# Four graph layers on one core: a POOL clear behind row gathers and scatters, and other chunk orders

## The chip, the core and the metric

The kernel runs on one core of a Trainium2 chip. A core has five engines with queues of their own: PE (TensorE, matrix products), DVE (VectorE), ACT (ScalarE), POOL (GpSimd) and SP (SyncE, which here only issues transfers). Transfers run on 16 DMA engines that all queues share. The metric is device time in microseconds (us) of one execution, as the median over runs.

## The reference

The input is a node matrix x of 3327 x 512 numbers and a 3327 x 3327 0/1 adjacency matrix with about four ones per row. Four layers follow each other; each normalises x, clips it at zero and adds what a graph layer makes of it:

```python
h = jnp.maximum(_layernorm(x, axis=-1), 0.0)
x = x + _L0_gnn_ref(h, adj, ...)   # mean of the neighbours' rows, two products, relu
h = jnp.maximum(_layernorm(x, axis=-1), 0.0)
x = x + _L1_gnn_ref(h, adj, ...)   # attention over neighbours, 8 heads of 64
h = jnp.maximum(_layernorm(x, axis=-1), 0.0)
x = x + _L2_gnn_ref(h, adj, ...)   # attention, 4 heads of 128, elu at the end
h = jnp.maximum(_layernorm(x, axis=-1), 0.0)
x = x + _L3_gnn_ref(h, adj, ...)   # attention, 1 head of 512
```

In an attention layer a node's score against each neighbour is a leaky relu of the sum of two numbers, one of each node; a softmax over the neighbours gives weights, and the node's new row is the weighted sum of the neighbours' projected rows.

## The kernel before

**The load stage** (plan of lines 880 to 1510) streams the adjacency matrix through SBUF, finds each row's ones (`L1209` on DVE), writes lists of neighbours (`records`, `L1261` to `L1267` on POOL), normalises x and multiplies it for layer 0, and sorts the nodes by number of neighbours. At its end 26 indirect transfers from POOL (`scatter`, `L1435`) write the rows in their sorted order to the DRAM table `own`; the records come back as `srec`, and the layers begin.

**The layers.** After the sort, the 3328 node places are 26 chunks of 128. Chunk 0 holds the nodes with most neighbours and has 14 slots, chunk 1 has 8, chunks 2 and 3 have 7, and so on down to chunks 24 and 25 with 1; 117 slots in all. For every slot of a chunk one indirect transfer (`gather`, `L1562`) fetches up to 128 rows of about 2 KB from the layer's DRAM table into the SBUF buffer `ring`, which has room for 33 slots. The table of the next layer is written by `project` (PE product `L1780`, ACT copies, an SP transfer), and no gather of a layer may start before all rows of its table have been written: a one-element clear on POOL (`mark`, `L2222`) waits for them.

Layer 0 sums slots on PE (`L1593`, a product with the identity) and DVE. Layers 1 and 2 compute scores on POOL (`L1942` clears padding, `L1950` adds two numbers for each slot and head), the softmax on DVE and ACT, multiply the slots by their weights in place (`L2138` on DVE, an operation that reads two SBUF operands; some slots on ACT), and sum on PE and DVE. Layer 3 takes its scores on DVE (`L1969`), makes the weighted sum there (`L2058`), projects on PE (`L2088`), and an indirect transfer from POOL (`L2100`) puts 128 finished rows of the output in their original places.

**What sets the order.** Inside the layers every engine's order is written out by a planner (class `Plan`). Each operation has an engine, an estimated cost in us, a rank and the operations it comes after; `run` simulates the engines as queues, takes whatever can start first, and emits the operations in order of their simulated start. The rank is the layer and the place of the chunk's unit in `ORDERS`, a hand-given list of single chunks and pairs for each layer. The engines then run strictly in that order. A gather costs 1.27 us in the planner, a clear of padding 0.15 us a chunk, and a score operation 0.3 us and more. The load stage is planned in the same way, but its last part, the scatters, is emitted after the plan and is placed by an automatic scheduler.

Of the kernel before, what the change touches and what calls it, by code (L numbers as in the profile page):

```python
# [8 lines left out]
F32 = mybir.dt.float32  # L9
# [9 lines left out]
P = 128  # L19
# [7 lines left out]
def general_path(  # L27
# [519 lines left out]
    def l3_finish(pc, i, o):  # L547
# [17 lines left out]
CAPS = tuple(-(-r // 128) for r in ROWS)  # L565
SEG = 4
RING = 33
NEVER = -1.0e30
LIFT = 0.5 ** (1.0 / 3.0)
LOG_LIFT = -0.23104906018664842  # L570
# [6 lines left out]

ORDERS = {
    0: (
        (24,), (12, 21), (11,), (6,), (18,), (17,), (15,), (4,), (3,), (20,), (5, 9), (22,), (10, 19), (1,),  # L580
        (2,), (14,), (0,), (23,), (8,), (13, 16), (7,), (25,),
    ),
    1: (
        (18, 21), (22, 24), (15,), (5,), (10, 20), (2,), (17,), (12, 23), (19,), (4,), (9, 14), (7,), (11, 16),
        (8, 13), (6,), (1,), (0,), (3,), (25,),
    ),
    2: (
        (18, 23), (19, 24), (16,), (20,), (6, 11), (10, 14), (7, 12), (5, 13), (9,), (1,), (21, 22), (4,), (0,),
        (8,), (2,), (3,), (15,), (17,), (25,),
    ),  # L590
    3: (
        (0,), (7,), (17,), (15, 20), (25,), (11,), (3,), (23,), (1, 5), (24,), (4, 14), (16,), (12, 22), (8,),
        (9,), (10,), (18,), (2,), (13,), (19,), (21,), (6,),
    ),
}

# [17 lines left out]
class Plan:  # L614
# [7 lines left out]
        self.limits = limits  # L622
        self.taker = {}

    def add(self, engine, cost, rank, emit=None, after=(), lag=0.0, take=(), give=()):
        op = {
            "engine": engine,
            "cost": cost,
            "rank": (rank, len(self.ops)),
            "emit": emit,  # L630
            "lag": lag,
            "take": take,
            "give": give,
            "need": 0,
            "ready": 0.0,
            "next": [],
        }

        after = list(after)
        for tag in take:  # L640
            if tag in self.taker:
                after.append(self.taker[tag])
            self.taker[tag] = op
        for a in after:
            a["next"].append(op)
            op["need"] += 1
        self.ops.append(op)
        return op

    def run(self):  # L650
        free = {}
        stock = {tag: [0.0] * n for tag, n in self.limits.items()}
        waiting = {}
        for op in self.ops:
            if not op["need"]:
                waiting.setdefault(op["engine"], []).append(op)
        order = []
        while any(waiting.values()):
            best = None
            for engine, ops in waiting.items():  # L660
                for op in ops:
                    at = max(op["ready"], free.get(engine, 0.0))
                    for tag in op["take"]:
                        at = max(at, min(stock[tag])) if stock[tag] else None
                        if at is None:
                            break
                    if at is not None and (best is None or (at, op["rank"]) < best[:2]):
                        best = (at, op["rank"], op)
            at, _, op = best
            waiting[op["engine"]].remove(op)  # L670
            for tag in op["take"]:
                stock[tag].remove(min(stock[tag]))
            op["at"] = at
            end = at + op["cost"]
            free[op["engine"]] = end
            for tag in op["give"]:
                stock[tag].append(end + 0.1)
            for after in op["next"]:
                lag = op["lag"] + (0.1 if after["engine"] != op["engine"] else 0.0)
                after["ready"] = max(after["ready"], end + lag)  # L680
                after["need"] -= 1
                if not after["need"]:
                    waiting.setdefault(after["engine"], []).append(after)
            order.append((at, len(order), op))
        assert len(order) == len(self.ops)
        for _, _, op in sorted(order, key=lambda o: o[:2]):
            if op["emit"]:
                op["emit"]()
        return max(free.values())
# [3 lines left out]
def gnn_stack_kernel(  # L693
# [19 lines left out]
    nc = tc.nc  # L713
# [21 lines left out]
    with ExitStack() as st:  # L735
# [116 lines left out]
        with tc.tile_pool(name="p0", bufs=1) as pa, tc.tile_pool(name="p0p", bufs=2, space=PSUM) as pp:  # L852
# [52 lines left out]
            fidx = pa.tile([P, NK, SEG * 8], U32, tag="fidx", name="fidx")  # L905
# [5 lines left out]
            plan = Plan(limits)  # L911
# [368 lines left out]
            for pos, i in enumerate(SEQUENCE):  # L1280
                found_of[i] = look(pos, i)
                for a, b in LISTED:
                    if i == max(range(a, b), key=pos_of.get):
                        done, rec = lists((ADJ * (pos + 0.9), 1), a, b, [f for k in range(a, b) for f in found_of[k]])
# [147 lines left out]
            landed = []  # L1432

            def scatter(i):
                ins = nc.gpsimd.indirect_dma_start(  # L1435
                    out=own,
                    out_offset=bass.IndirectOffsetOnAxis(ap=box["ranki"][:, i : i + 1], axis=0),
                    in_=node(i),
                    in_offset=None,
                )  # L1440

                for other in scattered:
                    tc.declare_no_dep(ins.ins, other.ins, reason="rows of their own")
                scattered.append(ins)
# [15 lines left out]
            with nc.allow_non_contiguous_dma(reason="each node's record and place beside its row"):  # L1460
# [46 lines left out]

                with tc.manual_schedule():
                    plan.run()
                for i in SEQUENCE:  # L1510
                    scatter(i)
                back()
                degrees()


        with tc.tile_pool(name="run", bufs=1, reuse_waits="tile") as pr, tc.tile_pool(
            name="runp", bufs=2, space=PSUM, reuse_waits="tile"
        ) as pp:
            xres = pr.tile([P, NK, D], F32, tag="xres", name="xres")
            ring = pr.tile([P, RING, WIDE], F32, tag="ring", name="ring")  # L1520
            hsum = {
                layer: pr.tile([P, NK, DC], F32, tag=f"hsum{layer}", name=f"hsum{layer}") for layer in (1, 2, 3)
            }
# [11 lines left out]
            def held(i, s):  # L1535

                return min(P, ROWS[s] - i * P)

            def pool_cost(m):
                return 1.27  # L1540
# [4 lines left out]
            def gather(layer, i, rank, barrier):  # L1545

                S = slots_of[i]
                r0 = ring_at[0] if ring_at[0] + S <= RING else 0
                ring_at[0] = r0 + S
                before = ring_readers[r0 : r0 + S]  # L1550
                last = []
                ring_readers[r0 : r0 + S] = [last] * S
                landed = []
                for s in range(S):

                    def emit(s=s):
                        if layer == 0:
                            idx = srec[:, i, s : s + 1]
                        else:
                            idx = nbr[:, base_of[i] + s : base_of[i] + s + 1]  # L1560
                        m = held(i, s)
                        nc.gpsimd.indirect_dma_start(  # L1562
                            out=ring[:m, r0 + s, : width[layer]],
                            out_offset=None,
                            in_=table[layer],
                            in_offset=bass.IndirectOffsetOnAxis(ap=idx[:m, :], axis=0),
                        )

                    after = barrier + before[s]
                    issue = plan.add("pool", pool_cost(held(i, s)), rank, emit, after)  # L1570
                    landed.append(plan.add("dma", 0.95 * held(i, s) / P, rank, None, [issue], lag=1.3))
                return ring[:, r0 : r0 + S, :], landed, last

# [337 lines left out]
            def attend(layer, number, unit, barrier):  # L1911
# [15 lines left out]
                if soft:  # L1927
# [14 lines left out]
                                nc.gpsimd.memset(e[:, j, full:, :], NEVER)  # L1942

                    if on_pool:
                        score = [plan.add("pool", 0.15 * n, rank, emit, take=("soft",))]
                        for j, i in enumerate(soft):
                            for lo, hi, m in runs_of(i, 0, slots_of[i]):

                                def emit(j=j, i=i, lo=lo, hi=hi, m=m, g=g, box=box):
                                    nc.gpsimd.tensor_tensor(  # L1950
                                        box["e"][:m, j, lo:hi, :],
                                        g[i][:m, lo:hi, D : D + H],
                                        fsrc[layer][:m, i, :].unsqueeze(1).to_broadcast([m, hi - lo, H]),
                                        ALU.add,
                                    )

                                score.append(
                                    plan.add("pool", 0.3 + 0.0015 * (hi - lo) * H, rank, emit, score[:1] + landed[i][lo:hi])
                                )

                    def emit(unit=soft, n=n, S=S, g=g, box=box, small=small, on_pool=on_pool):
# [58 lines left out]
                for j, i in enumerate(unit):  # L2020
# [56 lines left out]
                    if layer == 3:  # L2077
# [28 lines left out]
                                oob_is_err=False,  # L2106
                            )

                        issue = plan.add("pool", 1.3, rank, emit, [done])
                        plan.add("dma", 1.1, rank, None, [issue], lag=1.3, give=("t",))  # L2110
                        continue
                    j = unit.index(i)
# [121 lines left out]
                for number, unit in enumerate(ORDERS[layer]):  # L2234
                    ends += attend(layer, number, unit, barrier)
            with tc.manual_schedule():
                plan.run()


    general = nc.values_load(  # L2240
# [47 lines left out]
```

## Time and profile before

| | |
|---|---|
| median of 13 runs | 1110.13 us (1104.35 to 1112.82) |
| profiled execution | 1109.94 us, of which the span of the trace is 1107.9 us |
| busy, share of the span | PE 79%, DVE 65%, POOL 58%, ACT 47% |
| first gather, layer 0 to 3 | 268.58, 451.78, 680.50, 903.83 us |
| end of the last gather, layer 0 to 3 | 414.89, 635.07, 871.72, 1080.49 us |
| `mark` of layers 1 to 3 | 447.32, 676.50, 903.11 us |

Times inside the trace count from the first instruction. In the list of groups, the numbers after the bar are the busy time of the group, the mean time of one instruction in ns, the time the engine stood idle just before such instructions, and what ended most of that idle time; "issue" there means that the engine waited for nothing that the profile shows. In the list of waits, the three numbers are the total, the number of waits and the longest. In a timeline the numbers are start and duration in us, with idle time before the instruction in brackets.

### The profile page before, as it was taken

What the parts mean: (1) busy time and instruction counts of PE and PEld (TensorE: products, weight loads), DVE (VectorE), ACT (ScalarE), POOL (GpSimd) and SP (SyncE); (2) the same over time, 40 slices, a digit from 0 to 9 for tenths busy, and PEclk for the clock granted to TensorE, in tenths of its full rate; (3) what the DMA queues carried; (4) which work ended last, traced back from release to release, by engine and by line L of the source; (5) the groups of instructions that cost most, each with busy time, mean ns of one, the idle gap of its engine ahead of it and who ended that gap; (6) DMA issues with size and microseconds to landing.
All of it is one profiled execution on the core that took longest, in us unless ns stands there. A gap on an engine that the chain in (4) does not pass through costs nothing. (4 is left out here: it accounts for less than half of the span.)

```text
span 1107.9 us, 11566 instructions
## 1 busy us (share of the span) xinstructions
PE 880.7 (79%) x2853; PEld 498.2 (45%) x2853; DVE 716.4 (65%) x1760; ACT 519.9 (47%) x1700; POOL 643.3 (58%) x807
## 2 busy tenths in 40 slices
PE   7699999993999989388869693787889832949874
PEld 4244444441576757265636452444444431424332
DVE  6499988900869577287789491686767826536541
ACT  4398887530454435164657342455544631313231
POOL 1060444673777770577688703788767427777771
PEclk9899999996999999689999888688878955979988
DMA  9999888298999983467777603667656336677671
GB/s 352 316 355 388 303 304 296 88 358 297 303 335 325 320 273 120 130 181 195 201 193 197 181 30 98 184 179 195 185 159 184 112 102 171 203 201 210 193 209 55
DMA packets 89911, 240.51 MB, mean 217 GB/s; under 512 B 24933, under 2 KB 26477, under 8 KB 89834
## 3 DMA queue, kind: packets, MB, share of 16 engines
q0 software_dynamic: 41600, 137.72, 42.9%
q1 hardware_dynamic: 48234, 101.96, 26.0%
q8 instruction: 25, 0.41, 0.2%
q14 instruction: 52, 0.43, 0.1%
HBM read 190.35 MB, written 49.27 MB: 216 GB/s over the span
## 5 line engine op out<-in xcount | busy, mean ns | idle before, releaser
L1562 POOL DMA_INDIRECT ring<-table,nbr x351 | 379.1, 1080 | 114.4 <-issue 73.2
L1593 PE MATMUL acc<-ring,ident 128*128 128x512 f32 (+1 forms) x494 | 264.0, 671 | 81.3 <-DVE ring L2138 58.0
L1780 PE MATMUL pw<-w,hT 128*128 128x264 f32 (+1 forms) x832 | 195.0, 391 | 14.5 <-ACT hT L1705 14.5
L1780 PEld LDWEIGHTS pw<-w,hT 128*128 128x128 f32 x832 | 159.9, 193 | 55.2 <-ACT hT L1705 21.6
L1593 PEld LDWEIGHTS acc<-ring,ident 128*128 128x128 f32 (+1 forms) x494 | 96.9, 211 | 190.1 <-issue 81.4
L1562 POOL DMA_INDIRECT ring<-table,srec x117 | 111.0, 948 | 46.3 <-issue 20.7
L2138 DVE TENSOR_TENSOR ring<-ring,w 128x2048 f32<-128x2048 f32 (+7 forms) x76 | 114.6, 1534 | 1.7
L1209 DVE FIND_INDEX8 fidx<-one_i,ai 128x8 uint32<-128x832 int32 x104 | 104.2, 1019 | 0.0
L2088 PE MATMUL pw<-w,hT 128*128 128x512 f32 x208 | 96.7, 608 | 5.0 <-ACT hT L2080 5.0
L1217 ACT ACTIVATE junk<-ai 128x1664 int8<-128x1664 int32 (+1 forms) x52 | 82.7, 1591 | 33.0 <-DMA ai<-in_adj_dram 32.7
L1349 PE MATMUL pz_n<-wf,hT_n 128*128 128x512 f32 x208 | 92.3, 595 | 1.4 <-ACT hT_n L1342 1.4
L1349 PE MATMUL py_n<-wf,hT_n 128*128 128x512 f32 x208 | 91.9, 592 | 0.0
L1705 ACT ACTIVATE hT<-pt 128x128 f32<-128x128 f32 (+1 forms) x312 | 82.1, 292 | 19.3 <-PE pt L1694 18.7
L1996 ACT ACTIVATE ex<-el 128x48 f32<-128x48 f32 (+19 forms) x56 | 12.6, 228 | 134.1 <-DVE el L1979 133.7
L1976 DVE SCALAR_TENSOR_TENSOR el<-e 128x48 f32<-128x48 f32 (+19 forms) x56 | 10.3, 185 | 98.3 <-POOL e L1950 88.0
L1705 ACT ACTIVATION_READ_ACCUMULATOR hT<-pt 128x1 f32 x312 | 69.2, 223 | 0.0
L2088 PEld LDWEIGHTS pw<-w,hT 128*128 128x128 f32 x208 | 40.2, 196 | 60.0 <-issue 45.9
L1349 PEld LDWEIGHTS pz_n<-wf,hT_n 128*128 128x128 f32 x208 | 39.0, 190 | 51.1 <-issue 45.9
L822 ACT ACTIVATE ln<-mv,eps 128x1 f32<-128x1 f32 (+1 forms) x60 | 18.1, 302 | 92.9 <-DVE mv L1650 89.3
L2074 PE MATMUL pt<-ident,y 128*128 128x128 f32 x96 | 15.6, 294 | 57.9 <-DVE y L2058 51.5
L2124 ACT ACTIVATE ring<-ring,w 128x64 f32<-128x64 f32 (+1 forms) x216 | 57.7, 357 | 4.0 <-DVE w L2006 3.0
L2058 DVE SCALAR_TENSOR_TENSOR acc<-ring,w,acc 128x512 f32<-128x512 f32 (+2 forms) x67 | 50.5, 754 | 13.6 <-ACT acc L2056 12.0
(187 smaller groups left out, 1279.0 us busy)
## 6 DMA issues: line engine op xcount, KB each, us to landing
ai<-in_adj_dram SPq DMA_DIRECT2D x25, 832.0 KB, 7.1
ai<-in_adj_dram SPq DMA_DIRECT2D x25, 831.5 KB, 7.5
table<-t SPq DMA_DIRECT2D x52, 258.0 KB, 3.2
xy<-own SPq DMA_DIRECT2D x26, 512.0 KB, 5.7
table<-t SPq DMA_DIRECT2D x26, 260.0 KB, 5.7
table<-zt_n SPq DMA_DIRECT2D x26, 256.0 KB, 6.0
ring<-table,nbr POOLq DMA_INDIRECT x351, 3.7
later<-in_x_dram SPq DMA_DIRECT2D x15, 256.0 KB, 6.8
```

The lines of the kernel that those rows point to most:

```text
L822: nc.scalar.activation(ln, var, AF.Ln, bias=eps, scale=scale)
L1209: nc.vector.max_index(fidx[:, i, qq * 8 : (qq + 1) * 8], one_i, ai[:, q * QW : min(cols, (q + 1) * QW)])
L1217: nc.scalar.activation(junk[:, :cols], tiles["ai", key][:, :cols], AF.Square, accum_out=sq[:, i, hf : hf + 1])
L1349: nc.tensor.matmul(pz, tiles["hT", key][:, c, :], wf[s][:, c, :], start=(c == 0), stop=(c == DC - 1))
L1562: nc.gpsimd.indirect_dma_start(out=ring[:m, r0 + s, : width[layer]], out_offset=None, in_=table[layer], in_offset=bass.IndirectOffsetOnAxi ...
L1593: nc.tensor.matmul(acc, ident[:m, :], g[:m, s, :D], start=(k == 0), stop=(k == len(slots) - 1))
L1705: nc.scalar.activation(hT[:, c, :n], pt[:, c, :n], AF.Copy, accum_out=hsum[layer][:, i, c : c + 1])
L1780: nc.tensor.matmul(pw[:, b, :w], tiles["hT", key][:, c, :], wsb[layer][:, c, b, :w], start=(c == 0), stop=(c == DC - 1),)
L2058: nc.vector.scalar_tensor_tensor(to[:m, :], row, weight, acc[:m, :], ALU.mult, ALU.add)
L2088: nc.tensor.matmul(pw[:, 0, :], tiles["hT", key][:, c, :], w3[:, c, :], start=False, stop=(c == DC - 1))
L2124: nc.scalar.activation(v, v, AF.Copy, scale=box["w"][:m, j, s, h : h + 1])
L2138: nc.vector.tensor_tensor(v, v, box["w"][:m, j, lo:hi, :].unsqueeze(3).to_broadcast([m, hi - lo, H, O]), ALU.mult,)
```

## The change

1. A clear of an SBUF tile of 128 x 384 float32 numbers that nothing reads (`spacer`, `GAP`) is emitted on POOL between two operations of the layers' plan that are marked `spaced` and follow each other on POOL: row gathers, and the output's scatters of layer 3. Where a score operation stands between two gathers, no clear is put in.
2. In the source each scatter of the load stage is followed by a clear of the first 12 chunks' part of `fidx`, which has 384 numbers a partition.
3. The planner's cost of a gather or an output scatter goes up by 0.26 us (`SPACE`), and its costs of padding clears and scores on POOL go down.
4. `ORDERS` of all four layers are other permutations with other pairs. Every chunk's own instructions, slots and shapes stay the same.

```diff
+SPACE = 0.26
+GAP = 384
 ORDERS = {
     0: (
-        (24,), (12, 21), (11,), (6,), (18,), (17,), (15,), (4,), (3,), (20,), (5, 9), (22,), (10, 19), (1,),
-        (2,), (14,), (0,), (23,), (8,), (13, 16), (7,), (25,),
+        (24,), (16,), (11,), (21,), (22,), (23,), (7, 18), (20,), (0,), (13, 9), (12,), (6,), (14,), (17,),
+        (19,), (2,), (5,), (4,), (10,), (8,), (15,), (1,), (3,), (25,),
     1: (
-        (18, 21), (22, 24), (15,), (5,), (10, 20), (2,), (17,), (12, 23), (19,), (4,), (9, 14), (7,), (11, 16),
-        (8, 13), (6,), (1,), (0,), (3,), (25,),
+        (3, 22), (13,), (7,), (24,), (12,), (16,), (14, 5), (21,), (19, 20), (2,), (4,), (8,), (17, 23),
+        (18, 9), (6, 11), (0,), (10, 15), (1,), (25,),
     2: (
-        (18, 23), (19, 24), (16,), (20,), (6, 11), (10, 14), (7, 12), (5, 13), (9,), (1,), (21, 22), (4,), (0,),
-        (8,), (2,), (3,), (15,), (17,), (25,),
+        (12, 19), (9,), (22,), (23,), (2,), (14,), (21,), (8,), (7,), (5,), (18, 20), (6,), (11, 15), (13,),
+        (1,), (17,), (16,), (24,), (0,), (3,), (4,), (10,), (25,),
     3: (
-        (0,), (7,), (17,), (15, 20), (25,), (11,), (3,), (23,), (1, 5), (24,), (4, 14), (16,), (12, 22), (8,),
-        (9,), (10,), (18,), (2,), (13,), (19,), (21,), (6,),
+        (4,), (7, 24), (14,), (1,), (15,), (17, 13), (23,), (16,), (2, 19), (11,), (0,), (22,), (6,), (3,),
+        (12,), (5, 20), (18, 25), (9, 21), (8,), (10,),
...
-    def run(self):
+    def run(self, space=None):
...
+        behind = False
         for _, _, op in sorted(order, key=lambda o: o[:2]):
+            if op["engine"] == "pool":
+                if behind and op["spaced"]:
+                    space()
+                behind = op["spaced"]
             if op["emit"]:
                 op["emit"]()
...
+                gap = fidx[:, : GAP // 32, :].bitcast(F32)
                 for i in SEQUENCE:
                     scatter(i)
+                    nc.gpsimd.memset(gap, 0.0)
...
+            spacer = pr.tile([P, GAP], F32, tag="spacer", name="spacer")
...
-                    issue = plan.add("pool", pool_cost(held(i, s)), rank, emit, after)
+                    issue = plan.add("pool", pool_cost(held(i, s)) + SPACE, rank, emit, after, spaced=True)
...
-                        score = [plan.add("pool", 0.15 * n, rank, emit, take=("soft",))]
+                        score = [plan.add("pool", 0.05 * n, rank, emit, take=("soft",))]
...
-                                    plan.add("pool", 0.3 + 0.0015 * (hi - lo) * H, rank, emit, score[:1] + landed[i][lo:hi])
+                                    plan.add("pool", 0.1 + 0.0015 * (hi - lo) * H, rank, emit, score[:1] + landed[i][lo:hi])
...
-                        issue = plan.add("pool", 1.3, rank, emit, [done])
+                        issue = plan.add("pool", 1.3 + SPACE, rank, emit, [done], spaced=True)
...
-                plan.run()
+                plan.run(lambda: nc.gpsimd.memset(spacer, 0.0))
```

More of the change, by code (lines that the diff above doesn't have):

```diff
@@ L623, in __init__, with add @@
         self.taker = {}
-    def add(self, engine, cost, rank, emit=None, after=(), lag=0.0, take=(), give=()):
+    def add(self, engine, cost, rank, emit=None, after=(), lag=0.0, take=(), give=(), spaced=False):
         op = {
+            "spaced": spaced,
             "engine": engine,
```

## The prediction

> **What bounds the kernel now.** I read the page's groups first, for the line that the change touches, then the list of waits, then busy time cut at the gather windows, and last POOL's timeline.
>
> From the page, and from the list of waits:
>
> ```profile
> L1562 POOL DMA_INDIRECT ring<-table,nbr x351 | 379.1, 1080 | 114.4 <-issue 73.2
> L1562 POOL DMA_INDIRECT ring<-table,srec x117 | 111.0, 948 | 46.3 <-issue 20.7
> ```
>
> ```profile
> ACT ex L1996 <- DVE el L1979: 133.7, 30, 23.1
> POOL mark L2222 <- DMA table<-t: 100.8, 3, 40.0
> POOL ring L1562 <- issue: 94.0, 307, 2.2
> ...
> DVE el L1976 <- POOL e L1950: 88.0, 17, 19.1
> ...
> DVE e L1969 <- DMA ring<-table,nbr: 65.5, 17, 21.2
> ```
>
> The gathers' own idle time is almost all "issue": nothing visible holds them back. The others wait for them: DVE's scores for POOL's sums (88.0) and for landed rows (65.5), ACT for those scores. POOL's one long wait is the mark at each layer's end, three times, 40.0 us at most.
>
> Busy time by windows: each layer from its first to its last gather (columns: stretch, length, then busy us and instructions of each engine):
>
> ```profile
> 268.00:415.00 147.00, 135.36 (x510) 89.91 (x511) 109.44 (x250) 60.69 (x273) 111.06 (x118) 0.96 0.94 310
> 452.00:635.00 183.00, 138.38 (x526) 94.00 (x526) 130.41 (x294) 100.67 (x449) 140.22 (x158) 0.91 0.69 189
> 680.00:872.00 192.00, 152.87 (x462) 79.56 (x463) 128.46 (x277) 92.40 (x368) 148.07 (x159) 0.80 0.65 178
> 904.00:1081.00 177.00, 119.42 (x333) 56.64 (x334) 86.71 (x239) 44.42 (x90) 133.08 (x140) 0.84 0.69 197
> ```
>
> POOL looks three quarters busy, but its timeline shows that the rest is a fixed pause between gathers:
>
> ```profile
> 269.88 0.97 POOL L1562 DMA_INDIRECT ring<-table,srec  x1 [0.30 <-issue]
> 271.15 0.95 POOL L1562 DMA_INDIRECT ring<-table,srec  x1 [0.30 <-issue]
> 272.41 0.95 POOL L1562 DMA_INDIRECT ring<-table,srec  x1 [0.30 <-issue]
> ```
>
> One gather after another takes 0.95 + 0.30 = 1.255 us. Layer 0 is exactly that: 117 gathers from 268.58 to 414.89 are 146.3 us, 1.25 each. So 146.3 + 183.3 + 191.2 + 176.7 = 697.5 us of the span run at POOL's pace, and four ends, from a layer's last gather to the next layer's mark or to the end of the trace (32.4, 41.4, 31.4 and 27.4 us), run at the pace of PE, DVE and the table's writes. The page's chain of waits covers only the last store and says nothing of this.
>
> **The change part by part.** The built order of the changed kernel has 415 clears of `spacer`: 116 in layer 0, 83 in layer 1, 74 in layer 2, 142 in layer 3, of which 138 stand before its last gather. 411 therefore lie in the windows. Scores on POOL are 64 as before, outputs 26, gathers 468.
>
> *One clear.* No 128x384 clear is in the trace. The clear of 128x1040 takes 0.956 us and those of 128x8 take 0.12, so 384 by the line between them takes 0.12 + 376 x 0.81 ns = 0.42 us. How a clear sits between two gathers is shown here:
>
> ```profile
> 589.24 0.91 POOL L1562 DMA_INDIRECT ring<-table,nbr  x1 [0.30 <-DVE nra L831]
> 590.15 0.12 POOL L1942 MEMSET e<- 128x8 f32 x1
> 590.45 1.17 POOL L1562 DMA_INDIRECT ring<-table,nbr  x1 [0.19 <-issue]
> ```
>
> Start to start is 1.21 us: part of the pause is hidden behind the clear. The seven such places with an undelayed gather lie at 1.19 to 1.255, middle 1.22. With a clear longer by 0.30 that is 1.52, or 0.26 us more than two gathers in a row. The bounds: 1.19 + 0.30 gives 0.23; a score operation of 0.21 us between two gathers gives 1.345 start to start where it waits for nothing, and with 0.42 in its place 1.555, so 0.30. A gain would need a shorter gather; its place is with the rivals. I take 0.26, since a clear is the nearest row. Each new clear also waits for the clear before it, over a microsecond old by then: no cost.
> 411 x 0.26 = 106.9 us: layer 0 30.2, layer 1 21.6, layer 2 19.2, layer 3 35.9. Nothing hides it in the windows, as POOL has no other idle time there.
>
> *Stalls behind DVE's products.* Gathers keep POOL busy for 131.4 and 136.9 us in the windows of layers 1 and 2; 234 x 0.95 is 222.3, so 46 us are more than they need. The cause stands in the timelines of DVE and POOL:
>
> ```profile
> 554.57 2.29 DVE L2138 TENSOR_TENSOR ring<-ring,w 128x2048 f32<-128x2048 f32 x1
> ```
>
> ```profile
> 554.95 2.73 POOL L1562 DMA_INDIRECT ring<-table,nbr  x1 [0.30 <-issue]
> ```
>
> A gather that starts during a product of two SBUF operands ends 0.82 us after that product, never earlier; products keep their time. The clear at 590.15 took its 0.12 us inside a product that ran from 589.57 to 590.79, so a clear passes. Where the next gather would stall anyway, the clear is free: 36 gathers right behind a gather lasted over 1.3 us; of the 173 pairs of gathers in a row in these two layers 157 now get a clear, so some 33 x 0.26 = 8.5 us less. Against this, 15.0 us of products fell into the ends of layers 1 and 2; if half moves into the slower windows at the 46 us of stall per 100 us of product seen there, 3.5 more. Net -5. Bounds: -8.5, and +10 if all 15 move and the clear has to wait too.
>
> The Trainium skill ("SBUF — State Buffer", Who interferes with whom) says that such a DVE instruction holds up only GpSimd instructions that read SBUF, not those that only write; by this the clear passes as the row shows. The skill's "DMA: Bandwidth & Descriptors" (Anatomy of one DMA) puts the dispatch at about 50 ns and descriptor generation at small: by that POOL would have room, the clears would cost nothing and the sum would be about 0. The rows of 0.95 + 0.30 us for each gather decide against it here.
>
> *New orders.* They move no work between engines; they can only change fill and ends. Layer 0's end is PE's backlog: 135.36 of 147 us busy, then busy through to the mark. Thirty more microseconds of window remove it, and what stays is the last chunk: landing 4.8 us after its gather, then 16.0 us from its first sum on PE (431.36) to the mark (447.32), 20.8 instead of 32.4: -11 (bounds -14 and -5). Layer 1's end had the 14-slot chunk 0 and 7-slot chunk 3 last; now chunk 0 stands 18 gathers before the end, and chunks 10, 15 and 1 follow. Its end should come near layer 2's 31.4: -8 (-13 to 0). Layer 2 now ends with 6 and 5 slots instead of 4 and 3: 0 (-6 to +4). Layer 3 ends with a 5-slot chunk instead of 6 slots, one DVE step (0.75 us) less: -1 (-3 to +3). Sum -20. The first gather of a layer still waits for the same writes.
>
> *The scatters' clears.* In the built order they do not stand between the scatters: the scheduler puts 11 before or among the second group of records and 15 before the clears for the last adjacency rows. POOL idles 25.00 us before the one and 23.88 before the other; 26 x 0.42 = 10.9 us fit in there. The order of the other engines is the same up to layer 0's first chunks. Cost 0; without that cover 11 us. SP's queue issues the same transfers; no queue is passed by a longer one.
>
> *Sum.* 106.9 - 5 - 20 = +82 on the profiled execution's 1109.94 us, which is 0.2 below the median: **1192 us**.
>
> **The rivals.**
> *Clears spare the gathers their stalls.* Counted in POOL's timeline, of the 62 gathers right behind another POOL operation only 2 lasted over 1.3 us, of 406 behind a gather 36, with 44.7 us beyond 0.95. If the clear works like that, 44.7 x 157/173 = 41 us go, and the hidden clears of -5 do not come on top: 106.9 - 20 - 41 = +46, 1156 us. Against it: after a product starts, the next gather's start is later by 0.26 at most, less than most products' 1.2 to 2.3 us.
> *Faster: a spaced gather is itself shorter.* If a gather's 0.95 us contains a wait for the previous one's work, a clear would absorb it. Break-even is 82/411 = 0.20 us, a gather of 0.75. At 0.65, 411 x 0.30 = 123 less gives 1069 us. Against it: gathers behind another POOL operation last the same 0.95, and the shortest of all 468 is 0.867.
> *The scatters' clears are not covered*, the change not doing what it says: records and the last adjacency loads come 11 us later, 1203 us.
>
> **How the numbers follow.** The sum above 0.80, spared stalls 0.10, load stage late 0.04, shorter gathers 0.06. The likeliest one's own range: the clear's bounds move it by -12 and +16, the stalls by -3 and +15, the ends by -16 and +15 (not all at once), so 1165 to 1220. To hold 8 in 10 with the spared stalls partly in, 1150 to 1225. A difference under 0.2% can't be told from none here; slower 0.92, within 0.2% 0.02, faster 0.06.
>
> **What would show it.** POOL start to start about 1.52 us in layer 0, whose window grows from 146 to about 176 us, with a group of 415 clears near 0.42 us each; windows of about 203, 209 and 212 us in layers 1 to 3; layer 0's end near 21 us; the first gather still near 268.6. A gather mean in layers 1 and 2 near 0.95 would show spared stalls; gathers below 0.9 in layer 0 would make the forecast wrong, as would a window of layer 0 that stays at 146.

## The result, and the profile after

The changed kernel takes **1198.34 us** (median of 14 runs, 1194.62 to 1202.40) against 1110.42 us for the kernel before (median of 62, all but one of 1251.67 between 1104.35 and 1117.72): a ratio of **1.0791, 95% interval 1.0776 to 1.0806**, or 88 us more. Some runs of a kernel are some per cent slower than the rest, and the ratios, here and below, leave these out, so that they can differ a little from the quotient of two medians. The forecast was 1192 us in 1150 to 1225, slower with a chance of 0.92. The profiled execution took 1202.02 us, of which the span is 1199.9; the one of before took 1109.94 and 1107.9, so the traces differ by 92.0 us.

The page of the changed kernel, groups by line (busy us and mean ns of one, then idle time before them): the gathers are no longer than they were, and a new group of clears stands beside them.

```profile
L1573 POOL DMA_INDIRECT ring<-table,nbr x351 | 374.0, 1065 | 76.3 <-issue 54.0
...
L2248 POOL MEMSET spacer<- 128x384 f32 x415 | 180.7, 435 | 0.2
...
L1573 POOL DMA_INDIRECT ring<-table,srec x117 | 111.8, 955 | 31.5 <-issue 15.2
```

POOL's timeline at the start of layer 0 (start and duration in us; in brackets the idle time before):

```profile
268.94 0.97 POOL L1573 DMA_INDIRECT ring<-table,srec  x1 [0.16 <-issue]
269.91 0.43 POOL L2248 MEMSET spacer<- 128x384 f32 x1
270.50 0.96 POOL L1573 DMA_INDIRECT ring<-table,srec  x1 [0.16 <-issue]
```

One gather to the next is now 0.96 + 0.43 + 0.16, about 1.555 us, where it was 1.255: the clear takes 0.435 and gives about 0.135 of the pause back. So each clear costs **0.30 us** (median start to start in layer 0: 1.554 against 1.258).

Busy time of the engines in the windows from a layer's first gather to its last (columns as in the view of before: stretch, length, then PE, PEld, DVE, ACT, POOL, granted clock, DMA share, GB/s):

```profile
267.00:450.00 183.00, 161.10 (x592) 105.23 (x593) 124.04 (x287) 72.06 (x321) 162.12 (x235) 0.95 0.84 265
472.00:676.00 204.00, 144.85 (x532) 98.08 (x533) 135.31 (x291) 102.41 (x458) 175.81 (x241) 0.85 0.63 170
720.00:925.00 205.00, 155.38 (x474) 83.77 (x475) 136.65 (x321) 97.99 (x390) 173.38 (x229) 0.78 0.62 169
955.00:1174.00 219.00, 125.18 (x337) 58.46 (x338) 87.90 (x241) 45.46 (x90) 193.98 (x279) 0.80 0.57 159
```

The windows are longer in all four layers. DVE's and ACT's work in layer 3 is as before (88 against 87 us, 45 against 44) and PE's nearly so (125 against 119, at a granted clock of 0.80 against 0.84); POOL's rose from 133 to 194. In layer 0 PE issues 592 instructions inside the window where it issued 510: its backlog shrank, so the end after the last gather is shorter. By exact times from the trace:

| us | before | after | clears in it x 0.30 | measured |
|---|---|---|---|---|
| first gather | 268.58 | 267.35 | | -1.2 |
| window, layer 0 | 146.31 | 182.47 | 116: 34.8 | +36.2 |
| window, layer 1 | 183.29 | 202.76 | 83: 24.9 | +19.5 |
| window, layer 2 | 191.22 | 204.91 | 74: 22.2 | +13.7 |
| window, layer 3 | 176.66 | 217.93 | 138: 41.4 | +41.3 |
| end, layer 0 to 3 | 32.43, 41.43, 31.39, 27.41 | 16.16, 40.45, 29.99, 26.40 | | -19.7 |
| mark to first gather, layers 1 to 3 | 4.46, 4.00, 0.72 | 6.73, 4.12, 0.67 | | +2.3 |

Sum +92.1, the difference of the spans within rounding. The list of waits says the same from the other side: the marks stand less (67.3 us in two waits and 16.0 in a third, against 100.8), and what hangs on POOL's sums and on landed rows stands longer (ACT 162.6 against 133.7, DVE 104.5 against 88.0 and 108.4 against 65.5):

```profile
ACT ex L2007 <- DVE el L1990: 162.6, 36, 20.6
...
DVE e L1980 <- DMA ring<-table,nbr: 108.4, 22, 18.6
...
DVE el L1987 <- POOL e L1961: 104.5, 19, 24.5
...
POOL ring L1573 <- issue: 69.2, 391, 0.8
...
POOL mark L2233 <- DMA table<-t: 67.3, 2, 37.7
```

### The profile page after: what moved, and what is told of

Same layout as the page of the kernel before. It is cut to its first block, busy times and chain, and to the rows that moved or that the text cites. A ratio compares the mean times of both kernels' runs of the same rounds, so it can differ in the third digit from the quotient of the medians.

```text
span 1199.9 us, 12031 instructions
## 1 busy us (share of the span) xinstructions
PE 897.6 (75%) x2853; PEld 505.7 (42%) x2853; DVE 723.3 (60%) x1796; ACT 525.7 (44%) x1714; POOL 827.3 (69%) x1244
## 5 line engine op out<-in xcount | busy, mean ns | idle before, releaser
L1573 POOL DMA_INDIRECT ring<-table,nbr x351 | 374.0, 1065 | 76.3 <-issue 54.0
L1604 PE MATMUL acc<-ring,ident 128*128 128x512 f32 (+2 forms) x494 | 269.4, 683 | 128.2 <-DVE ring L2149 90.3
L1604 PEld LDWEIGHTS acc<-ring,ident 128*128 128x128 f32 (+2 forms) x494 | 98.0, 215 | 242.4 <-DVE ring L2149 99.6
L1791 PE MATMUL pw<-w,hT 128*128 128x264 f32 (+1 forms) x832 | 192.3, 387 | 4.1 <-ACT hT L1716 2.3
L2248 POOL MEMSET spacer<- 128x384 f32 x415 | 180.7, 435 | 0.2
L2007 ACT ACTIVATE ex<-el 128x32 f32<-128x32 f32 (+21 forms) x58 | 12.9, 226 | 162.6 <-DVE el L1990 162.6
L1987 DVE SCALAR_TENSOR_TENSOR el<-e 128x32 f32<-128x32 f32 (+21 forms) x58 | 10.7, 184 | 105.4 <-POOL e L1961 104.5
L1980 DVE TENSOR_TENSOR e<-ring,fs 128x4 f32<-128x4 f32 (+10 forms) x32 | 5.0, 160 | 112.1 <-DMA ring<-table,nbr 108.4
L1814 ACT COPY t<-pw 128x512 f32<-128x512 f32 (+1 forms) x54 | 30.5, 564 | 68.5 <-PE pw L1791 62.6
```

Source lines behind the costliest of these rows:

```text
L1573: nc.gpsimd.indirect_dma_start(out=ring[:m, r0 + s, : width[layer]], out_offset=None, in_=table[layer], in_offset=bass.IndirectOffsetOnAxi ...
L1604: nc.tensor.matmul(acc, ident[:m, :], g[:m, s, :D], start=(k == 0), stop=(k == len(slots) - 1))
L1791: nc.tensor.matmul(pw[:, b, :w], tiles["hT", key][:, c, :], wsb[layer][:, c, b, :w], start=(c == 0), stop=(c == DC - 1),)
L1814: nc.scalar.copy(t[:, :D].rearrange("p (b f) -> p b f", b=2)[:, lo:hi, :], pw[:, lo:hi, :HD])
L2248: plan.run(lambda: nc.gpsimd.memset(spacer, 0.0))
```

## The experiments

Ten kernels ran in twelve runs, on three chips. On the first the kernel before took 1109.13 us (17 runs); on the second 1195.33 (7) and on the third 1212.84 (19). That difference has a part below. Totals are compared only with the kernel before on the same chip; windows and periods of different chips are set side by side where the text says so. The change itself was measured where the kernel before takes 1110.

### 1. The clears of the layers alone

The kernel before, with its orders and planner's costs, plus the hook and its clear; nothing in the load stage.

```diff
+            spacer = pr.tile([P, 384], F32, tag="spacer", name="spacer")
-                    issue = plan.add("pool", pool_cost(held(i, s)), rank, emit, after)
+                    issue = plan.add("pool", pool_cost(held(i, s)), rank, emit, after, spaced=True)
-                plan.run()
+                plan.run(lambda: nc.gpsimd.memset(spacer, 0.0))
```

> The kernel before with its own orders and planner costs, and only the clears of 128x384 put in behind gathers and output scatters in the layers (none in the load stage); 417 of them lie in the four gather windows. Theory 'pace' (POOL's queue paces the windows, a clear makes two gathers start 1.555 us apart instead of 1.255): 417 x 0.30 = 125 us more in the windows, of which about 14 are hidden under DVE's products and 17 are given back at the layers' ends, so about 1204 us, near the changed kernel's 1198. Theory 'orders' (a large part of the 88 us comes from the new orders and planner costs): clearly less than 1198, about 1150. Third possibility, the orders were worth something with the clears in: 1210 or more.

First chip: **1206.11 us**, ratio 1.0861 (1.0830 to 1.0893). The page's group of the clears:

```profile
L2244 POOL MEMSET spacer<- 128x384 f32 x421 | 183.4, 436 | 0.2
```

The windows are 182.39, 196.13, 205.35 and 216.56 us: +103.0 for the 417 clears in them, where 417 x 0.30 would be 125. Layers 0 and 3 pay in full (+36.1 and +39.9 for 34.8 and 41.4), layers 1 and 2 only +12.8 of 25.5 and +14.1 of 23.4. Layer 0's end falls to 23.84 without any new order. The clears alone make more than the whole loss (97 us), and the rest of the change is worth some 8 us of gain on top of them (1206.11 to 1198.34; the intervals of the two ratios do not overlap).

### 2. The orders and costs alone

The changed kernel without a single clear.

```diff
-                    nc.gpsimd.memset(gap, 0.0)
-                plan.run(lambda: nc.gpsimd.memset(spacer, 0.0))
+                plan.run(lambda: None)
```

> The changed kernel with its orders and planner costs but without any clear, neither in the layers nor in the load stage. 'Pace': the windows fall back to 1.255 us a gather, layer 0's window to 146 to 148 us, total within 10 us of the kernel before, 1100 to 1120. 'Orders': 1150 us or more, with layer windows longer than before though no clear stands in them.

First chip: **1142.39 us**, ratio 1.0298 (1.0264 to 1.0331). Neither theory had this right: the windows of layers 0 to 2 are back at 146.32, 181.95 and 191.26, as the pace says, but the kernel is 33 us slower than before. Layer 0's end is 41.65 (+9.2), and layer 3's window is 199.02 (+22.4). One wait has grown in layer 3. In the kernel before (whole span), and in this one (from 940 us on):

```profile
POOL out_dram L2100 <- ACT t L2095: 11.5, 3, 4.8
```

```profile
POOL out_dram L2108 <- ACT t L2103: 35.1, 19, 4.3
```

and POOL's timeline at one of these places:

```profile
1046.07 0.95 POOL L1570 DMA_INDIRECT ring<-table,nbr  x1 [0.30 <-issue]
1047.32 0.91 POOL L1570 DMA_INDIRECT ring<-table,nbr  x1 [0.30 <-issue]
1052.10 1.02 POOL L2108 DMA_INDIRECT out_dram<-t,srec  x1 [3.86 <-ACT t L2103]
1053.42 0.97 POOL L1570 DMA_INDIRECT ring<-table,nbr  x1 [0.30 <-issue]
```

POOL comes to an output scatter before its rows are ready, waits for ACT's `t`, and every gather behind waits too. A likely reading is that the planner put the scatter where a pace of 1.53 us a gather would have its rows ready, and that POOL at 1.25 comes there early; whether the new costs or the new lists place it so is not shown. The parts of the change do not add: with the clears in, the new orders and costs gain 8 us; without them they lose 33.

### 3. A clear of 8 numbers instead of 384

```diff
-                plan.run(lambda: nc.gpsimd.memset(spacer, 0.0))
+                plan.run(lambda: nc.gpsimd.memset(spacer[:, :8], 0.0))
```

> The changed kernel with each of the layers' clears cut from 384 to 8 numbers a partition; as many instructions on POOL as in the changed kernel, in the same places. 'Pace' by length: 0.96 + 0.12 + 0.17 = 1.25 us between starts, so the same as without clears, 1100 to 1120 us. If the mere presence of an instruction costs (its dispatch, its wait on the clear before): 30 to 60 us above that.

First chip: **1142.83 us**, ratio 1.0305 (1.0278 to 1.0331), the time of experiment 2. The expected 1100 to 1120 was missed by what experiment 2 had already shown: the orders and costs lose 33 us. Group and timeline:

```profile
L2248 POOL MEMSET spacer<- 128x8 f32 x415 | 50.7, 122 | 0.2
```

```profile
281.42 0.96 POOL L1573 DMA_INDIRECT ring<-table,srec  x1 [0.18 <-issue]
282.38 0.12 POOL L2248 MEMSET spacer<- 128x8 f32 x1
282.69 0.96 POOL L1573 DMA_INDIRECT ring<-table,srec  x1 [0.18 <-issue]
```

Start to start is 1.264: 415 clears of 0.12 us, 50.7 us of POOL's time, cost nothing that the total shows, as the pause after a gather shrinks by nearly as much. What costs is a clear's length beyond that, not its presence. This kernel also keeps the 26 clears of the load stage, which experiment 2 leaves out: the first gather comes at 268.73 us here and at 268.15 there, so they do not lengthen the load stage by anything near 26 x 0.43 = 11 us.

### 4. A clear of one number in the kernel before

Before's orders and costs; each clear writes its own column, so that none waits for another.

```diff
+            spacer = pr.tile([P, 448], F32, tag="spacer", name="spacer")
+            column = iter(range(448))
+            def space():
+                k = next(column)
+                nc.gpsimd.memset(spacer[:, k : k + 1], 0.0)
-                plan.run()
+                plan.run(space)
```

> The kernel before, own orders and costs, with a clear of one number a partition behind gathers and output scatters, each in a column of its own, so that no clear waits for another. The seven padding clears of the kernel before, which wait for nothing, had starts 1.22 us apart where gathers in a row have 1.255. If that 0.035 to 0.04 us is real and the windows are at POOL's pace: 417 x 0.04 = 17 us less, of which 2 to 4 are lost at layer 0's end, so 1095 to 1098 us, faster than both kernels. If it is only how the records overlap: 1110.

First chip: **1110.45 us**, ratio 1.0013 (0.9995 to 1.0032): the same. The hoped-for gain did not come. The timeline shows a period of 1.255, not the 1.21 that the prediction had read from padding clears:

```profile
280.31 0.95 POOL L1575 DMA_INDIRECT ring<-table,srec  x1 [0.19 <-issue]
281.25 0.12 POOL L1532 MEMSET spacer<- 128x1 f32 x1
281.56 0.95 POOL L1575 DMA_INDIRECT ring<-table,srec  x1 [0.19 <-issue]
```

This run settles how the prediction's 0.26 went wrong, below.

### 5. A clear of 192 numbers

```diff
+                plan.run(lambda: nc.gpsimd.memset(spacer[:, :192], 0.0))
```

> The changed kernel with each of the layers' clears cut to 192 numbers a partition. 'Pace': a clear of 0.27 us makes starts 0.96 + 0.27 + 0.17 = 1.40 us apart, so the four windows together lie 411 x 0.155 = 64 us below the changed kernel's, less what comes back at layer 0's end and at layer 3's output scatters, which wait again: 1150 to 1165 us. If the pace is set by something that a short clear already triggers: near the changed kernel's 1198 or near 1143 with a step between.

This one ran on the second chip: **1210.4 us** against 1195.33 there, ratio 1.0125 (1.0065 to 1.0184). The period is readable whatever the chip: 0.96 + 0.27 + 0.16, a median of 1.396 us. With 1.264 for 8 numbers and 1.555 for 384, a clear costs its length beyond about 0.12 to 0.14 us. The total says nothing of the first chip, for which 1150 to 1165 was expected.

### 6. A copy that reads SBUF in place of the clear

```diff
+                plan.run(lambda: nc.gpsimd.tensor_copy(spacer[:, :COPY], biasf[:, :COPY]))   # COPY = 256
```

> The changed kernel with a POOL copy of 256 numbers a partition from one SBUF tile to the spacer in place of each of the layers' clears, chosen to last about as long (0.40 to 0.45 us). 'Clears hide under DVE's products because they only write': layers 0 and 3 as in the changed kernel, windows of layers 1 and 2 each 5 to 12 us longer, with copies that last up to 2.5 us, total 1205 to 1220. If reading makes no difference: 1195 to 1202.

Second chip: **1220.35 us**, ratio 1.0199 (1.0147 to 1.0251). Between gathers of layer 0 a copy takes 0.41 us and the period is 1.545, so it stands in for the clear. Its group has a longer mean:

```profile
L2249 POOL COPY spacer<-biasf 128x256 f32<-128x256 f32 x415 | 206.1, 497 | 1.9
```

The difference lies under DVE's products. The timelines of DVE and POOL with the copy:

```profile
506.47 1.76 DVE L2150 TENSOR_TENSOR ring<-ring,w 128x1536 f32<-128x1536 f32 x1
...
506.61 1.87 POOL L2249 COPY spacer<-biasf 128x256 f32<-128x256 f32 x1
```

and in the changed kernel with the clear (four products in a row from 491.85):

```profile
491.85 4.62 DVE L2149 TENSOR_TENSOR ring<-ring,w 128x2048 f32<-128x2048 f32 x4
...
492.19 0.44 POOL L2248 MEMSET spacer<- 128x384 f32 x1
```

The copy that starts under a product ends 0.25 us after it, as all 29 such copies do; the clear keeps its 0.44, and none of the 32 clears that start under a product takes longer. In layers 1 and 2 the copies take 55.1 and 46.4 us, the clears 36.1 and 32.2, and the windows are 10.1 and 8.7 us longer than the changed kernel's, measured on another chip; in layers 0 and 3 they are about as long as its own (181.48 and 217.09). So POOL's operation that reads SBUF is held up and the one that only writes is not. That is what the Trainium skill says ("SBUF — State Buffer", Who interferes with whom): a DVE instruction with two SBUF inputs contends with a GpSimd instruction that reads SBUF, not with one that only writes.

### 7 and 8. New orders with old costs; old orders with new costs

Both without clears, to split the 33 us of experiment 2. They ran twice, on the second and on the third chip, and never on the first.

```diff
 ORDERS = { ... }        # 7: the new permutations in the kernel before
-                    issue = plan.add("pool", pool_cost(held(i, s)), rank, emit, after)
+                    issue = plan.add("pool", pool_cost(held(i, s)) + SPACE, rank, emit, after)   # 8, and the other new costs
```

> The kernel before with the new lists of chunks alone: planner costs of before, no clears. Lists and costs together had cost 33 us without clears, 22 of them in layer 3's window, where POOL stood before output scatters until ACT had copied their rows. If the costs are at fault (the planner thinks 1.53 us a gather, places an output scatter as many gathers behind as that allows, and the chip reaches it early), layer 3's window is back at 177 us and the total near 1120. If the lists are, it stays near 199 and 1142.

> The new orders of chunks with the planner's old costs and no clears. Theory 'orders cost': the new orders alone make the kernel longer where no clears space the gathers, and the 33 us of the run without clears come from them: on a chip where the kernel before takes 1110 us, this one takes 1135 to 1145, with a first end of about 40 us and a last window of about 199. Rival 'costs cost': the orders alone are worth nothing or a little gain, 1100 to 1115. On a chip where the kernel before takes 1195 us, 1227 as before.

> The other half: the lists of before with the planner's new costs, no clears. If the costs are at fault for layer 3: its window near 199 us, total 1130 to 1135. If the lists are: 177 us and 1110. Layer 0's end (32.4 us before, 41.7 with lists and costs both new) goes with whichever half has it.

> The old orders with the planner's costs raised by 0.26 us for each gather, and no clears. Theory 'orders cost': the planner only lays the other work out for a pace that does not come, 1110 to 1118 us on a chip where the kernel before takes 1110. Rival 'costs cost': 1130 to 1145 us there, with POOL waiting at the scatters or the output of the last layer. On a chip where the kernel before takes 1195 us, 1240 as before.

New orders alone: **1226.9 us**, ratio 1.0275 (1.0201 to 1.0348) on the second chip, and 1247.26, ratio 1.0345 (1.0266 to 1.0424) on the third. New costs alone: **1239.5**, 1.0333 (1.0256 to 1.0409), and 1257.58, 1.0401 (1.0257 to 1.0545). On these chips each alone loses 32 to 45 us. But there the kernel before itself takes 86 to 104 us more, so these ratios mix two causes, and the losses lie elsewhere than in experiment 2. With the new orders alone layer 2's end is 57.4 and 58.3 us, where experiment 2 has 31.75 and the kernel before on the third chip 32.25. Layer 3's window is 199.1 and 204.5 us, the expected 199 if the lists were at fault; but on the third chip the kernel before has 204.3 itself, with 42.0 us of POOL's wait for ACT's `t` against 11.5 where it takes 1110. Which half makes the 33 us on the first chip stays open.

### 9 and 10. The kernel before unchanged, and the change without the scatters' clears, on the third chip

The second chip's 1195 us for the kernel before asked for its trace. Run 9 is that kernel unchanged. Run 10 is the changed kernel without the load stage's clears:

```diff
-                gap = fidx[:, : GAP // 32, :].bitcast(F32)
-                    nc.gpsimd.memset(gap, 0.0)
```

> The kernel before, unchanged, for its trace on this chip. Two kinds of chip have been met: one where it takes 1109 to 1110 us and one where it took 1195 us. Theory 'chip': the 85 us between them lie in pauses of POOL among close gathers, above all in the first layer, so on a chip of the second kind the first layer's window is about 190 us or more instead of 146 and the load stage as long as ever (first gather near 268 us). Rival 'DMA is slower there': the load stage is longer as well, and SP's transfers take longer from issue to their last packet (median of xy on the first chip 5.5 us). On a chip of the first kind: 1110 us, ratio 1.000, windows of 146, 183, 191 and 177 us.

> The changed kernel without the clears behind the first scatters; the clears in the layers stay. By the prediction these cost nothing, since POOL waits for VectorE there: the same time as the changed kernel within 3 us, 1195 to 1202 us on a chip where the kernel before takes 1110 (ratio 1.077 to 1.083), and a first gather within 2 us of 267.4. A rival, that they stand in the path of the load stage: 26 x 0.43 = 11 us less, 1187 us and a first gather near 256.

Third chip: the kernel before **1214.45 us** (ratio 1.0029 to itself, 0.9969 to 1.0088), and the one with the layers' clears **1205.25 us**, ratio **0.9976 (0.9935 to 1.0016)**: no difference that can be measured. On this chip the layers' clears, with the new orders and costs, cost nothing in all. Busy time of the kernel before there, layer 0's window and end and the windows of layers 1 and 3:

```profile
278.00:464.00 186.00, 125.52 (x448) 83.24 (x448) 95.30 (x220) 52.31 (x235) 110.95 (x118) 0.83 0.75 238
464.00:517.00 53.00, 49.06 (x203) 35.53 (x204) 35.23 (x85) 25.04 (x118) 0.05 (x1) 1.00 0.27 95
521.00:705.00 184.00, 140.24 (x526) 95.49 (x526) 130.44 (x294) 101.05 (x449) 142.60 (x159) 0.89 0.66 188
974.00:1179.00 205.00, 129.23 (x322) 59.35 (x323) 86.54 (x239) 42.28 (x87) 133.04 (x139) 0.79 0.58 170
```

and of the one with clears, layers 0 and 3:

```profile
275.00:458.00 183.00, 160.17 (x600) 105.48 (x601) 125.05 (x289) 73.23 (x329) 162.13 (x235) 0.97 0.84 265
957.00:1175.00 218.00, 127.55 (x335) 59.64 (x336) 88.07 (x241) 45.15 (x90) 193.44 (x277) 0.79 0.55 160
```

Of the 99.6 us by which the kernel before is longer here than where it takes 1110 (spans 1207.5 and 1107.9), 9.7 lie in the load stage (first gather at 278.24 instead of 268.58), 39.4 in layer 0's window, 20.9 in its end, 27.6 in layer 3's window, and under 1 in each of the windows of layers 1 and 2. Layers 0 and 3 are those whose gathers follow each other most closely. With clears the windows of layers 0 and 3 are 182.48 and 217.94 us here, and 182.47 and 217.93 on the chip where the change was measured. So 88 of the 99.6 us lie in layer 0 and in layer 3's window, and they are not there when the gathers are spaced. The theory had named layer 0 above all, with a window of 190 us or more. POOL does stand longer in layer 0, 39.6 us beyond its fixed pauses where the profile of before has none, but the trace puts about half of that down to waits for PE and DVE. The longer load stage that the rival asked for is there too, with 9.7; it lies in the 26 indirect scatters at its end, which start within 49.6 us instead of 37.0, while the first of them starts at 219.4 us instead of 219.7. The new orders and costs together, without clears, did not run on this chip; experiments 7 and 8 show that neither alone removes the loss.

For the scatters' clears run 10 says little, since the changed kernel was not run on this chip. Its first gather, at 275.27 us, misses the expected 267.4 with the chip's longer load stage; the four kernels without these clears that ran here lie between 275.27 and 278.24. Experiments 2 and 3 are the better test.

## Why the prediction was right

**The bound and its cost.** The reading that the windows run at POOL's pace, pause included, carried the forecast: 102.95 us of windows for clears alone (experiment 1), and DVE's and ACT's work in layer 3 did not grow. The pause hides a clear only up to about 0.12 to 0.14 us (experiments 3 to 5).

The Trainium skill's "DMA: Bandwidth & Descriptors" (Anatomy of one DMA) calls descriptor generation small. These runs do not agree with it for such gathers: each holds POOL for 0.95 us, and the next one starts 0.30 later.

**The clear's 0.26, the term that was mis-sized.** It is 0.30, the upper bound, given by the row of the score operation. The step that failed is "The seven such places with an undelayed gather lie at 1.19 to 1.255, middle 1.22". I read the low values as a pause that the clear makes shorter in all; they were shorter gathers. The gathers just before those padding clears have 32, 64 or 96 rows but for one, and the one of 128 rows has the 1.255. In the trace of before the gathers sort by rows: a median of 0.875 us for 32 rows (20 of them), 0.914 for 64 (20), 0.929 for 96 (4), 0.952 for 128 (424). The quoted gather at 589.24 took 0.91. Experiment 4 shows the clean case: a clear of 0.12 us between 128-row gathers leaves the period at 1.255. 411 x 0.04 = 16 us more than predicted.

**The clear's length.** The line from 8 to 1040 numbers gave 0.42; it measured 0.435.

**Stalls.** Net -5 was predicted. By windows, 411 x 0.30 = 123.3 came out as 110.6, so -12.7, all of it in layers 1 and 2 (-5.4 and -8.5); in experiment 1 it was -22. The mechanism, a clear that takes its time under a product or a wait that is there anyway, is seen in the rows of experiment 6; its size was set too low. In layers 1 and 2 together POOL's gathers took 262.7 us instead of 268.6 and its waits beyond the fixed pause 11.7 instead of 14.1; the rest of the 13.9 is not told apart. One reading was too strong: of the 51 gathers of before that start under a product, 50 end after it but one ends 1.4 us earlier, so "never earlier" does not hold. The two misses, +16 and -8, partly cancel, which is luck.

**The ends.** Predicted -20, measured -19.7; that the sums agree is luck, since the places do not: layer 0 -16.3 instead of -11, layer 1 -1.0 instead of -8, layer 2 -1.4, layer 3 -1.0. Layer 0's -16.3 is 8.6 from the longer window alone (experiment 1: 23.84) and 7.7 from the new order. For layer 1 the step "Its end should come near layer 2's 31.4" failed: it stayed at 40.45, and in experiment 1 with the old order 40.52. The 2.3 us more from the first mark to the first gather of layer 1 were not in the sum.

**New orders: "they can only change fill and ends".** With clears this held well enough; without them it does not. Together with the planner's costs the orders set where POOL's scatters and gathers stand against PE and ACT, and experiment 2 shows 22.4 us inside layer 3's window from that. I treated the costs as neutral and did not ask which pace the order was laid out for.

**The scatters' clears.** Cost 0, as predicted. The trace of after has them before the second group of records and before the adjacency clears; POOL's waits there:

```profile
POOL fidx L1521 <- DVE low L1245: 21.2, 1, 21.2
...
POOL ai L1208 <- DMA ai<-in_adj_dram: 14.4, 1, 14.4
```

The wait for adjacency rows fell from 23.9 to 14.4 us, so the clears took time in which POOL would have waited. The first gather came at 267.35 instead of 268.58, a difference no larger than that between kernels with the same load stage (266.48 to 268.58 in four of them, on the first chip or where before takes 1110).

**The rivals.** *Spared stalls*: refuted. 452 of the 468 gathers now stand behind another POOL operation, and 34 still last over 1.3 us, where 38 did. *Shorter gathers*: refuted: 0.96 us behind a clear of 384. *Load stage late*: refuted by the first gather, and by experiments 2 and 3. What no rival had: the price of the orders without the clears, and the chips.

## What to carry to other kernels

Measure an engine's pace from start to start, pause included, and price an inserted instruction by rows with the same neighbours: here a shorter gather beside the clear looked like overlap and made the price an eighth too low. An order written out by a planner belongs to the pace it was planned for; test orders and pace together, since here the same orders and costs gained 8 us at one pace and lost 33 at the other. And look at the kernel on more than one chip: a change that cost 88 us on one cost nothing measurable, but for the load stage's clears, on another.

## What the runs showed of the hardware that I had not expected

**A short clear between two gathers is free.** 421 clears of 0.12 us moved 1109.13 to 1110.45 us, within what can be measured.

**The number of rows hardly matters to a gather's time on POOL.** 0.875 us for 32 rows, 0.952 for 128.

**On two of the three chips the kernel before took 86 to 104 us more, and with gathers 1.55 us apart the loss is gone from the windows.** Each chip was met in one set of runs, so the chip and the moment can't be told apart. The granted clock does not explain it: it is 0.866 for the kernel before on the third chip and 0.867 for the changed kernel where before takes 1110, and PE's mean matmul takes 476 ns on the third chip against 467. The timeline of the kernel before on the third chip, DVE and ACT early in layer 0, and then DVE's next instruction:

```profile
297.20 0.17 DVE L1862 CAST nbr<-ring 128x4 int32<-128x4 f32 x1
...
318.93 0.58 ACT L1803 COPY t<-pw 128x512 f32<-128x512 f32 x1 [26.68 <-issue]
```

```profile
329.43 0.76 DVE L1871 SCALAR_TENSOR_TENSOR acc<-acc,rdeg,xy 128x512 f32<-128x512 f32 x1 [32.05 <-remote]
```

POOL meanwhile goes on at its pace:

```profile
307.18 0.95 POOL L1562 DMA_INDIRECT ring<-table,srec  x1 [0.30 <-issue]
308.44 0.95 POOL L1562 DMA_INDIRECT ring<-table,srec  x1 [0.30 <-issue]
```

ACT waits 26.7 us for PE's semaphore, though by the trace the last product for this copy ended at 295.4. DVE's 32 us end with PE too: the trace has an update of PE's semaphore at 329.40, 30.0 us after the end that it gives for the last matmul before (299.43; the ends of matmuls are modelled there). SP issues nothing between the `xy` transfer by 296 and 319.6, and from 305 to 320 no packet of its queue moves, while the gathers' packets do.

The table counts, from 265 us on, pauses of more than 2 us of PE, DVE, ACT or POOL whose end the trace can't explain ("issue" or "remote"), and updates of PE's semaphore that come over 1 us after the end of the last matmul that makes one:

| chip, kernel | gather start to start, us | such pauses | us in all | late updates of PE |
|---|---|---|---|---|
| first: one number; 8 numbers; no clears | 1.258; 1.264; 1.257 | 7; 8; 7 | 22; 24; 22 | 1; 1; 1 |
| where before takes 1110: before; changed kernel | 1.257; 1.554 | 7; 7 | 22; 34 | 1; 1 |
| second: new orders; new costs, no clears | 1.26 | 43; 43 | 287; 272 | 47; 46 |
| third: before; new orders; new costs | 1.26 | 43; 50; 42 | 302; 297; 246 | 43; 59; 50 |
| second: clear of 192 | 1.396 | 25 | 127 | 27 |
| second: copy | 1.545 | 7 | 33 | 1 |
| third: clears of 384 | 1.552 | 10 | 42 | 1 |

On the two slow chips the pauses fall as the gathers are spaced out, and at 1.55 us they are about as few as on the first. Of the 17 pauses marked "remote" in the kernel before on the third chip 15 end with such a late update. SP's transfers, once issued, are not slower there: with packets matched to transfers by bytes, an `xy` transfer reaches its last packet 4.4 us after its issue in the kernel before on the third chip, and 4.8 in the profile that the prediction used (medians). So slower `xy` transfers are not the cause in the layers. Nor does code that comes late fit the two pauses shown: no packet of the instruction queues moves between 300.4 and 342.1 us, while ACT and DVE start again at 318.93 and 329.43. Whether PE's products ended late or were only told late, no run here separates.

One more thing is to be known of these counts. In the runs on the slow chips a part of the semaphore updates is missing from the trace, all of it after the first 200 us: for PE, DVE and ACT it has 2460 of the 3194 updates in the kernel before on the third chip and 2857 of 3264 with clears, where the runs on the first chip lack none. So a pause that nothing explains there may be one whose record is lost. The pauses themselves are real in the timelines: whatever ended them, those over 2 us come to 1232 us over the four engines in the kernel before on the third chip and to 858 where it takes 1110, and with clears of 384 to 1072 and 1050 on the same two. But every run on record comes with a span and a granted clock, so none is known to have gone unrecorded, and a rival stays untested: that the recording itself holds the engines up on these chips.
